# Edge places compared with the lanes on GpSimd, tile by tile behind the gathers, in a graph layer with a routed expert layer

## The chip, the cores and the metric

The kernel runs on one core of a Trainium2 chip. The metric is the device time of one execution in microseconds (us). The core has five engines that run side by side, each in its own program order: TensorE (PE in the profile), VectorE (DVE), ScalarE (ACT), GpSimd (POOL) and SyncE (SP, which here only issues DMAs).

## The reference

Inputs are 6,250 nodes `x` of 256 features, 100,000 edges (`src`, `dst`, sorted by `dst`, and two weights per edge), the weights of one graph layer and of eight experts, all float32. What the part around the change computes:

```python
h_fwd = h @ W_forward.T                 # h = layernorm(x); 64 features
h_rev = h @ W_reverse.T
messages = h_fwd[src] * direction[:, 0:1] + h_rev[src] * direction[:, 1:2]
scores = leaky_relu(einsum('ef,hf->eh', messages, attn))        # 4 heads
exp_scores = exp(scores - scores.max(axis=0))
sum_exp = segment_sum(exp_scores, dst)
norm = exp_scores / (sum_exp[dst] + 1e-10)
outs = [segment_sum(messages * norm[:, hd:hd + 1], dst) for hd in range(H)]
x = x + concatenation of outs           # 4 x 64 = 256 features
```

After it every node is normalized again, sent to one of eight experts by the largest of eight gate logits (with a limit on the nodes per expert), goes through a layer of 1,024 hidden units with ReLU, is weighted by its gate probability, and is added to `x`.

## The kernel before

**First stage (about 0 to 75 us).** The kernel normalizes the nodes, multiplies them by both weight matrices and stores a table of 6,250 rows of 136 floats in HBM (`node_tab`: for each direction 64 features and 4 head scores). It also transposes the edge data so that each column holds a tile of 128 edges, one per partition. `srci` holds the sources as integers; `local` holds, for each edge, the row of its destination within a window of up to 128 consecutive nodes (lines 813 and 814, through `less`). `lane` is a 128x128 tile with 0 to 127 along each row, and `lane_p` is a copy of it in PSUM, in the tile `fixed`.

**The edge stage (about 75 to 1170 us).** There are 782 edge tiles. They are taken in `NB` = 66 bursts of up to `GB` = 12 tiles, in the order of the list `order`. For each burst b:

- `gathers(b)` (line 985): one indirect DMA on GpSimd per tile (line 989) fetches 128 rows of `node_tab` into `gt`, which has three buffers. Between the gathers of a burst's second half it also issues scatters of routed rows (`put`, line 1198), if some are waiting in `pool_work`.
- `messages(b)` (line 995): VectorE multiplies both directions by their edge weights (lines 1004 and 1009), adds them (1011) and makes the scores; ScalarE takes the exponential (1024).
- `places(b)` (line 1027): VectorE compares `local` with the lanes, for all tiles of a burst in one instruction (line 1032). The result `hot` has a 1 where an edge's destination is that lane. It has two buffers.
- `products(b)` (line 1036): VectorE multiplies messages and exponentials for the four heads (line 1041).
- `windows(b, half)` (line 1052): PE multiplies `hot` with the products (line 1073), six tiles in each half, and accumulates in PSUM the sums for a window of nodes. ScalarE copies a finished window out (line 1077) and SyncE stores it into `sums`.

**The order of the work** is written out by hand: the loop at line 1461 builds every engine's program in the order of its calls. In iteration b it calls `messages(b)`, `windows(b-1, 0)`, a share of expert work, `places(b)`, `products(b)`, `windows(b-1, 1)`, another share of expert work, and at the end `gathers(b+3)`. In between, `step_routing` advances the routing of chunks of nodes whose sums are complete: it loads the sums again (line 1105), divides, adds, normalizes (1114 to 1128), finds the expert and the slot, and leaves scatters to GpSimd. `step_experts` calls the expert matmuls (lines 1351 and 1369) by a fixed share of estimated costs, so that how much expert work stands in an iteration is settled when the program is built.

**The tail (to the end)**: the remaining expert matmuls, and the gathers and stores of the outputs.

Operands of VectorE's large instructions lie in PSUM on one side (`fixed`, `rv`), so most of them have a single input in SBUF.

Of the kernel before, what the change touches and what calls it, by code (L numbers as in the profile page):

```python
# [8 lines left out]
F32 = mybir.dt.float32  # L9
I32 = mybir.dt.int32  # L10
AF = mybir.ActivationFunctionType
OP = mybir.AluOpType
AX = mybir.AxisListType

P = 128
# [504 lines left out]
def kernel(  # L520
# [27 lines left out]
    nc = tc.nc  # L548
# [14 lines left out]
    ROW = 2 * MS  # L563
# [6 lines left out]
    GB = 12  # L570
# [10 lines left out]
    GT = GB // 2  # L581
# [24 lines left out]
    node_tab = dram.tile([N, ROW], F32, name="node_tab")  # L606
# [38 lines left out]
    lane = const.tile([P, P], F32, name="lane")  # L645
# [55 lines left out]
    srci = ep.tile([P, EW], I32, name="srci")  # L701
    ea = ep.tile([P, 2, EW], F32, name="ea")
    local = ep.tile([P, ET], F32, name="local")
# [153 lines left out]
    def clear(r):  # L857

        nc.sync.dma_start(buf[r:r + 512, 0:D].rearrange("(p n) d -> p n d", n=4),
                          zeros.rearrange("p (n d) -> p n d", n=4))  # L860

    def clear_last(e):

        r0, r1 = e * TOT + OFF[NP - 2], (e + 1) * TOT
        J = (r1 - r0) // P
        nc.sync.dma_start(ybuf[r0:r1, :].rearrange("(p n) d -> p (n d)", n=J), zeros[:, 0:J * D])
        r0 = e * TOT + OFF[NP - 1]
        J = (r1 - r0) // P
        nc.sync.dma_start(buf[r0:r1, D:BW].rearrange("(p n) k -> p n k", n=J),
                          zeros[:, 0:J * (D + 2)].rearrange("p (n k) -> p n k", k=D + 2))  # L870
# [7 lines left out]
    order = [(i, min(i + GB, TOP)) for i in range(HEAD, TOP, GB)]  # L878
# [3 lines left out]
    NB = len(order)  # L882
# [59 lines left out]
    with tc.tile_pool(name="p4", bufs=1) as p4, tc.tile_pool(name="p5", bufs=2) as p5, \  # L942
# [3 lines left out]
        p2 = edge_pools.enter_context(tc.tile_pool(name="p2", bufs=2))  # L946
# [4 lines left out]
        lane_p, shift_p = fixed[:, 0:P], fixed[:, P:P + H]  # L951

        def turn(b, k0, k1):
            o = P + H + b % 2 * (2 + H) * GB
            return fixed[:, o + k0 * GB:o + k1 * GB]
# [23 lines left out]
            got.append(over)  # L979


        gts, vs = {}, {}
        pool_work = []

        def gathers(b):
            i0, i1 = order[b]
            gts[b] = p2.tile([P, GB, ROW], F32, name="gt", bufs=3)
            for i in range(i0, i1):
                nc.gpsimd.indirect_dma_start(  # L989
                    out=gts[b][:, i - i0, :], out_offset=None, in_=node_tab,  # L990
                    in_offset=bass.IndirectOffsetOnAxis(ap=srci[:, i:i + 1], axis=0))
                if i - i0 >= GT and pool_work:
                    pool_work.pop(0)()

        def messages(b):

            i0, i1 = order[b]
            n = i1 - i0
            gt = gts.pop(b)
            m = p2.tile([P, GB, MS], F32, name="m")  # L1000
            fac = turn(b, 0, 2).rearrange("p (k j) -> p k j", k=2)
            nc.vector.tensor_copy(fac[:, :, :n], ea[:, :, i0:i1])
            fw = gt[:, :n, 0:MS]
            nc.vector.tensor_mul(fw, fw, fac[:, 0, :n].unsqueeze(2).to_broadcast([P, n, MS]))  # L1004
            for a0 in range(0, n, GT):
                a1 = min(a0 + GT, n)
                k = a1 - a0
                rv = ps2.tile([P, GT, MS], F32, name="rv")
                nc.vector.tensor_mul(rv[:, :k, :], gt[:, a0:a1, MS:ROW],  # L1009
                                     fac[:, 1, a0:a1].unsqueeze(2).to_broadcast([P, k, MS]))  # L1010
                nc.vector.tensor_add(m[:, a0:a1, :], fw[:, a0:a1, :], rv[:, :k, :])  # L1011
            sc = p2.tile([P, GB, H], F32, name="sc")
            s = sc[:, :n, :]
            nc.vector.scalar_tensor_tensor(s, m[:, :n, O:MS], 0.2, m[:, :n, O:MS],
                                           op0=OP.mult, op1=OP.max)
            if i1 == ET:
                nc.vector.tensor_scalar(sc[:, n - 1, :], sc[:, n - 1, :], no_edge, None, op0=OP.add)
            nc.vector.tensor_reduce(gmax[:, b, :], s.rearrange("p j h -> p h j"), AX.X, OP.max)
            if b == 0:
                nc.vector.tensor_reduce(shift, spread(gmax[:, 0, :]), AX.X, OP.max)  # L1020
                nc.vector.tensor_copy(shift_p, shift)
            nc.vector.tensor_sub(s, s, shift_p.unsqueeze(1).to_broadcast([P, n, H]))  # L1022
            v = p2.tile([P, GB, ACC], F32, name="v")
            nc.scalar.activation(v[:, :n, H * O:ACC], s, AF.Exp)  # L1024
            vs[b] = m, v

        def places(b):

            i0, i1 = order[b]
            n = i1 - i0  # L1030
            hot = p2.tile([P, GB, P], F32, name="hot")
            nc.vector.tensor_tensor(hot[:, :n, :], lane_p.unsqueeze(1).to_broadcast([P, n, P]),  # L1032
                                    local[:, i0:i1].unsqueeze(2).to_broadcast([P, n, P]), OP.is_equal)
            vs[b] += (hot,)

        def products(b):
            n = order[b][1] - order[b][0]
            m, v, hot = vs[b]
            w = turn(b, 2, 2 + H).rearrange("p (j h) -> p j h", h=H)
            nc.vector.tensor_copy(w[:, :n, :], v[:, :n, H * O:ACC])  # L1040
            nc.vector.tensor_mul(  # L1041
                v[:, :n, 0:H * O].rearrange("p n (h o) -> p n h o", h=H),
                m[:, :n, 0:O].unsqueeze(2).to_broadcast([P, n, H, O]),
                w[:, :n, :].unsqueeze(3).to_broadcast([P, n, H, O]))

            vl = p2.tile([P, ACC], F32, name="vl")
            nc.scalar.copy(vl, v[:, n - 1, :])  # L1047
            vs[b] = v, hot, vl

        taken = {"released": 0, "passes": 0, "before": None, "pv": None, "rows": 0, "jobs": 0, "fetched": 0}  # L1050

# [376 lines left out]
        def routes_of(c):  # L1428
            nonlocal next_p
            for cost in route(c, next_p):  # L1430
                yield cost
            if chunks[c][-1] == LASTS[next_p]:
                end_pass(next_p)
                wait_pass.append(next_p)
                next_p += 1
                if next_p < NP:
                    begin_pass(next_p)
                yield 0.0

        def step_routing():  # L1440
            nonlocal credit
            while routing:
                cost = next(routing[0], None)
                if cost is None:
                    routing.pop(0)
                    continue
                credit -= cost
                break

        def step_experts(share):  # L1450
            nonlocal credit
            credit = min(credit + share, share)
            while credit > 0 and b > 12:
                cost = step_ffn()
                if cost is None:
                    break
                credit -= cost

        for b in range(3):
            gathers(b)  # L1460
        for b in range(NB + 1):
            if 4 <= b < 4 + E:
                clear(1024 * (b - 4))
                clear(1024 * (b - 4) + 512)
                clear_last(b - 4)
            if b < NB:
                messages(b)
            step_routing()
            if b:
                windows(b - 1, 0)  # L1470
            step_experts(SHARE / 2)
            step_routing()
            if b < NB:
                places(b)
            step_routing()
            if b < NB:
                products(b)
            step_routing()
            if b:
                windows(b - 1, 1)  # L1480
            taken["released"] = taken["rows"]
            step_experts(SHARE / 2)
            while next_c < len(chunks) and done_at[next_c] < b:
                routing.append(routes_of(next_c))
                next_c += 1
            step_routing()
            pool_work.extend(todo)
            del todo[:]
            if b + 3 < NB:
                gathers(b + 3)  # L1490
            if wait_pass and not pool_work:
                taken["rows"] = wait_pass.pop() + 1
                i = (taken["rows"] - 1) * E
                if taken["jobs"] >= i - 1:
                    fetch_rows(i)
                    fetch_rows(i + 1)
# [115 lines left out]
```

## Time and profile before

| what | value |
| --- | --- |
| median of 9 runs | 1452.01 us (1445.87 to 1457.55) |
| the profiled execution | 1448.44 us |
| its span in the profile | 1446.6 us |
| PE busy | 1085.1 us (75%) |
| VectorE busy | 971.6 us (67%) |
| GpSimd busy | 863.2 us (60%) |
| ScalarE busy | 306.5 us (21%) |
| granted TensorE clock, mean | 0.85 of full speed |

How to read what follows. A group of instructions stands in one line: source line, engine, operation, what it writes and reads, the count behind an x, then its busy time in us and the mean of one in ns, then how long its engine was idle just before such instructions and what ended most of that idle time. "issue" means that the profile shows nothing that the engine waited for. In a timeline each line has the start, the duration, the engine and instruction, and in brackets the idle time before it. A row of the waits has who waited for whom, the sum in us, how often, and the longest. In the row of 40 slices each digit is the busy share of one slice of about 36 us, in tenths.

### The profile page before, as it was taken

The page shows a single profiled execution, that of the slowest core. Times are in us where ns is not written, and L with a number is a line of the kernel's source. Part 1 is how long each engine was busy: PE and PEld are TensorE (multiplying, and loading weights), DVE is VectorE, ACT ScalarE, POOL GpSimd, SP SyncE. Part 2 cuts the span into 40 slices and gives each one's busy share as a digit, 9 for nine tenths or more (in the row PEclk, how much of TensorE's full clock was granted, in tenths as well). Part 3 has the DMA queues.
Part 4 walks back from the last instruction along what each step waited for, and adds up shares of the span by engine and source line. Part 5 has one row for each costly group of instructions (what it writes and reads, how often), then busy time and mean ns, then how long its engine had stood idle before and what let it go on. Part 6 is the DMA issues. An engine that isn't in the chain of part 4 may idle for free.

```text
span 1446.6 us, 15046 instructions
## 1 busy us (share of the span) xinstructions
PE 1085.1 (75%) x4658; PEld 867.8 (60%) x4658; DVE 971.6 (67%) x2062; ACT 306.5 (21%) x771; POOL 863.2 (60%) x912
## 2 busy tenths in 40 slices
PE   6815554647447561979897998797889998999885
PEld 5614443435325341767676776675768887888774
DVE  6836557587578584576969878779789744215772
ACT  3500000010011010222222222222222233224441
POOL 0067777777777777767777777775777502004414
PEclk9957677767767666989898898898879999999998
DMA  7422666563333343448466675765675456767992
GB/s 226 130 51 63 176 187 187 152 188 76 75 104 71 80 110 97 130 134 217 131 189 174 185 193 157 172 195 150 169 187 157 141 171 197 259 200 253 298 290 73
DMA packets 160583, 231.22 MB, mean 160 GB/s; under 512 B 19760, under 2 KB 130542, under 8 KB 160366
## 3 DMA queue, kind: packets, MB, share of 16 engines
q1 hardware_dynamic: 125354, 152.34, 33.4%
q0 software_dynamic: 32064, 75.13, 21.7%
q10 hardware_dynamic: 3076, 2.69, 0.6%
q8 instruction: 39, 0.64, 0.2%
q14 instruction: 50, 0.41, 0.1%
HBM read 167.19 MB, written 63.70 MB: 160 GB/s over the span
## 4 chain that ended last, share of the span: by engine, by line
PE 31%; POOL 21%; DVE 19%; DMA 16%; issue 11%; ACT 2%; SPq 0%; DVEq 0%; POOLq 0%; ACTq 0%
POOL gt L989 19%; PE ph L1351 8%; PE pv L1073 8%; PE py L1369 8%; DVE v L1041 4%; DMA part<-sums 4%; DMA sums<-r 3%; DMA gt<-node_tab,srci 2%; PE pn L783 2%; PE pl L1142 2%; DMA out_dram<-o 1%; DVE hot L1032 1%; DMA yg<-ybuf,to_get 1%; DVE ln_st L673 1%; DVE hx L1122 1%
## 5 line engine op out<-in xcount | busy, mean ns | idle before, releaser
L989 POOL DMA_INDIRECT gt<-node_tab,srci x782 | 747.6, 956 | 257.4 <-issue 234.4
L1073 PE MATMUL pv<-v,hot 128*128 128x260 f32 x1564 | 459.7, 447 | 132.8 <-DVE v L1041 126.2
L1073 PEld LDWEIGHTS pv<-v,hot 128*128 128x128 f32 x1564 | 337.4, 224 | 237.5 <-issue 179.5
L1351 PE MATMUL ph<-xT,w1t 128*128 128x256 f32 x1024 | 237.8, 385 | 6.8 <-DVE y L1277 6.2
L1369 PE MATMUL py<-w2t,hf 128*128 128x256 f32 x1024 | 228.6, 380 | 4.2 <-ACT hf L1354 4.2
L1041 DVE TENSOR_TENSOR v<-m,fixed 128x3072 f32<-128x3072 f32 (+1 forms) x66 | 218.7, 3313 | 2.3
L1351 PEld LDWEIGHTS ph<-xT,w1t 128*128 128x128 f32 x1024 | 197.7, 194 | 36.4 <-DVE y L1277 7.4
L1369 PEld LDWEIGHTS py<-w2t,hf 128*128 128x128 f32 x1024 | 192.2, 190 | 30.9 <-ACT hf L1354 5.9
L1004 DVE TENSOR_TENSOR gt<-gt,fixed 128x816 f32<-128x816 f32 (+1 forms) x66 | 65.6, 993 | 151.7 <-DMA gt<-node_tab,srci 144.4
L1354 ACT ACTIVATE hf<-ph,b1t 128x256 f32<-128x256 f32 x256 | 105.9, 470 | 187.3 <-PE ph L1351 187.1
L1401 POOL DMA_INDIRECT yg<-ybuf,to_get x49 | 48.6, 992 | 151.3 <-DMA xr<-x_d 80.1
L1032 DVE TENSOR_TENSOR hot<-fixed,local 128x1536 f32<-128x1536 f32 (+1 forms) x66 | 114.2, 1730 | 0.0
L1134 PE MATMUL pt<-ident,hx 128*128 128x128 f32 x98 | 23.5, 413 | 90.2 <-DVE hx L683 90.2
L1198 POOL DMA_INDIRECT buf<-hx,to_put x49 | 48.5, 990 | 68.6 <-DVE kept L1219 44.4
L1277 DVE TENSOR_TENSOR y<-py,b2b 128x512 f32<-128x512 f32 x32 | 22.0, 686 | 94.2 <-PE py L1369 94.2
L1024 ACT ACTIVATE v<-sc 128x48 f32<-128x48 f32 (+1 forms) x66 | 16.0, 242 | 313.4 <-DVE sc L1022 313.3
L1011 DVE TENSOR_TENSOR m<-gt,rv 128x408 f32<-128x408 f32 x131 | 75.5, 576 | 4.5
L1009 DVE TENSOR_TENSOR rv<-gt,fixed 128x408 f32<-128x408 f32 x131 | 76.1, 581 | 2.2
L1047 ACT COPY vl<-v 128x260 f32<-128x260 f32 x66 | 26.9, 407 | 235.6 <-DVE v L1041 175.6
L1134 PEld LDWEIGHTS pt<-ident,hx 128*128 128x128 f32 x98 | 17.9, 210 | 95.8 <-DVE hx L683 57.2
L1077 ACT COPY r<-pv 128x260 f32<-128x260 f32 x87 | 32.2, 370 | 115.6 <-PE pv L1073 115.6
L1142 PEld LDWEIGHTS pl<-gw,ht 128*128 128x128 f32 x196 | 42.5, 328 | 2.8 <-ACT ht L1136 2.7
(221 smaller groups left out, 894.3 us busy)
## 6 DMA issues: line engine op xcount, KB each, us to landing
w1t<-in_L_ffn_w_dram SPq DMA_DIRECT2D x32, 1024.0 KB
w2t<-in_L_ffn_w_dram SPq DMA_DIRECT2D x32, 1024.0 KB
gt<-node_tab,srci POOLq DMA_INDIRECT x782, 2.9
sums<-r SPq DMA_DIRECT2D x85, 125.9 KB
buf<-zeros SPq DMA_DIRECT2D x16, 512.0 KB
xe<-buf SPq DMA_DIRECT2D x32, 256.0 KB
part<-sums SPq DMA_DIRECT2D x12, 520.0 KB
x_d<-hx SPq DMA_DIRECT2D x12, 512.0 KB
```

Of the source, the lines that this page charges most:

```text
L989: nc.gpsimd.indirect_dma_start(out=gts[b][:, i - i0, :], out_offset=None, in_=node_tab, in_offset=bass.IndirectOffsetOnAxis(ap=srci[:, i:i ...
L1004: nc.vector.tensor_mul(fw, fw, fac[:, 0, :n].unsqueeze(2).to_broadcast([P, n, MS]))
L1009: nc.vector.tensor_mul(rv[:, :k, :], gt[:, a0:a1, MS:ROW], fac[:, 1, a0:a1].unsqueeze(2).to_broadcast([P, k, MS]))
L1011: nc.vector.tensor_add(m[:, a0:a1, :], fw[:, a0:a1, :], rv[:, :k, :])
L1032: nc.vector.tensor_tensor(hot[:, :n, :], lane_p.unsqueeze(1).to_broadcast([P, n, P]), local[:, i0:i1].unsqueeze(2).to_broadcast([P, n, P]) ...
L1041: nc.vector.tensor_mul(v[:, :n, 0:H * O].rearrange("p n (h o) -> p n h o", h=H), m[:, :n, 0:O].unsqueeze(2).to_broadcast([P, n, H, O]), w[ ...
L1073: nc.tensor.matmul(pv, hot[:, i - i0, :], v[:, i - i0, :], start=(i == g0), stop=(i == g1 - 1))
L1142: nc.tensor.matmul(pl[:, n, :], hts[n // 2][:, n % 2, d, :], gw[:, d, :], start=(d == 0), stop=(d == DC - 1))
L1351: nc.tensor.matmul(ph[:, f - f0, :], w1t[:, d, f * P:(f + 1) * P], xT[:, d, :S], start=(d == 0), stop=(d == DC - 1))
L1354: nc.scalar.activation(hf[:, f, :S], ph[:, f - f0, :], AF.Relu, bias=b1t[:, e * FC + f:e * FC + f + 1])
L1369: nc.tensor.matmul(py[:, j - j0, :], hf[:, f, j * P:(j + 1) * P], w2t[:, f, :], start=(f == 0), stop=(f == FC - 1))
L1401: nc.gpsimd.indirect_dma_start(out=yg[:, n, :], out_offset=None, in_=ybuf, in_offset=bass.IndirectOffsetOnAxis(ap=to_get[:, n0 + n:n0 + n ...
```

## The change

The comparison moves from VectorE to GpSimd. It is split into one instruction per tile, which reads `lane` from SBUF and one column of `local` as a scalar per partition. The comparisons of burst b-1 stand in `gathers(b)`, one behind each gather, so the places of a burst are made while the next burst is gathered. The tile `hot` gets four buffers in place of two. `gathers` is called one more time, with b = `NB`, for the places of the last burst alone. The call of `places` in the main loop goes, and `products` takes the places from a dictionary of their own.

```diff
         def gathers(b):
-            i0, i1 = order[b]
-            gts[b] = p2.tile([P, GB, ROW], F32, name="gt", bufs=3)
-            for i in range(i0, i1):
-                nc.gpsimd.indirect_dma_start(
-                    out=gts[b][:, i - i0, :], out_offset=None, in_=node_tab,
-                    in_offset=bass.IndirectOffsetOnAxis(ap=srci[:, i:i + 1], axis=0))
-                if i - i0 >= GT and pool_work:
-                    pool_work.pop(0)()
+            i0, i1 = order[b] if b < NB else (0, 0)
+            if b < NB:
+                gts[b] = p2.tile([P, GB, ROW], F32, name="gt", bufs=3)
+            for i in range(GB):
+                if i < i1 - i0:
+                    nc.gpsimd.indirect_dma_start(
+                        out=gts[b][:, i, :], out_offset=None, in_=node_tab,
+                        in_offset=bass.IndirectOffsetOnAxis(ap=srci[:, i0 + i:i0 + i + 1], axis=0))
+                    if i >= GT and pool_work:
+                        pool_work.pop(0)()
+                if b:
+                    places(b - 1, i)
...
-        def places(b):
+        def places(b, i):
             i0, i1 = order[b]
-            n = i1 - i0
-            hot = p2.tile([P, GB, P], F32, name="hot")
-            nc.vector.tensor_tensor(hot[:, :n, :], lane_p.unsqueeze(1).to_broadcast([P, n, P]),
-                                    local[:, i0:i1].unsqueeze(2).to_broadcast([P, n, P]), OP.is_equal)
-            vs[b] += (hot,)
+            if not i:
+                places_of[b] = p2.tile([P, GB, P], F32, name="hot", bufs=4)
+            if i < i1 - i0:
+                nc.gpsimd.tensor_scalar(places_of[b][:, i, :], lane, local[:, i0 + i:i0 + i + 1], None, op0=OP.is_equal)
...
-            vs[b] = v, hot, vl
+            vs[b] = v, places_of.pop(b), vl
...
-            if b < NB:
-                places(b)
...
-            if b + 3 < NB:
+            if b + 3 <= NB:
                 gathers(b + 3)
```

More of the change, by code (lines that the diff above doesn't have):

```diff
@@ L979, in term @@
             got.append(over)
-        gts, vs = {}, {}
+        gts, vs, places_of = {}, {}, {}
         pool_work = []
         def gathers(b):
-            i0, i1 = order[b]
-            gts[b] = p2.tile([P, GB, ROW], F32, name="gt", bufs=3)
-            for i in range(i0, i1):
-                nc.gpsimd.indirect_dma_start(
-                    out=gts[b][:, i - i0, :], out_offset=None, in_=node_tab,
-                    in_offset=bass.IndirectOffsetOnAxis(ap=srci[:, i:i + 1], axis=0))
-                if i - i0 >= GT and pool_work:
-                    pool_work.pop(0)()
+            i0, i1 = order[b] if b < NB else (0, 0)
[10 more added lines that the diff above has]
+                    places(b - 1, i)
         def messages(b):
@@ L1025, in messages @@
             vs[b] = m, v
-        def places(b):
+        def places(b, i):
             i0, i1 = order[b]
-            n = i1 - i0
-            hot = p2.tile([P, GB, P], F32, name="hot")
-            nc.vector.tensor_tensor(hot[:, :n, :], lane_p.unsqueeze(1).to_broadcast([P, n, P]),
-                                    local[:, i0:i1].unsqueeze(2).to_broadcast([P, n, P]), OP.is_equal)
-            vs[b] += (hot,)
+            if not i:
+                places_of[b] = p2.tile([P, GB, P], F32, name="hot", bufs=4)
+            if i < i1 - i0:
+                nc.gpsimd.tensor_scalar(places_of[b][:, i, :], lane, local[:, i0 + i:i0 + i + 1], None, op0=OP.is_equal)
         def products(b):
             n = order[b][1] - order[b][0]
-            m, v, hot = vs[b]
+            m, v = vs[b]
             w = turn(b, 2, 2 + H).rearrange("p (j h) -> p j h", h=H)
```

## The prediction

> **What bounds the kernel now.** I read the busy row of GpSimd over the 40 slices first, then the costliest groups, then GpSimd's own timeline, and last the waits, because the change puts 782 new instructions on one engine and the question is whether that engine has room.
>
> From the page: the slices, and the two groups that the change touches.
> ```profile
> POOL 0067777777777777767777777775777502004414
> ...
> L989 POOL DMA_INDIRECT gt<-node_tab,srci x782 | 747.6, 956 | 257.4 <-issue 234.4
> ...
> L1032 DVE TENSOR_TENSOR hot<-fixed,local 128x1536 f32<-128x1536 f32 (+1 forms) x66 | 114.2, 1730 | 0.0
> ```
> GpSimd is only about 75% busy from slice 3 to slice 29, which looks like room. The gather row says what the other quarter is: of 257.4 us idle ahead of the gathers, 234.4 are "issue", time in which the engine waited for nothing that the profile shows. The timeline of GpSimd alone shows its form (start, duration, idle before):
> ```profile
> 77.36 0.95 POOL L989 DMA_INDIRECT gt<-node_tab,srci  x1 [0.30 <-issue]
> 78.62 0.94 POOL L989 DMA_INDIRECT gt<-node_tab,srci  x1 [0.30 <-issue]
> 79.86 0.94 POOL L989 DMA_INDIRECT gt<-node_tab,srci  x1 [0.30 <-issue]
> ```
> A gather starts every 1.25 us, 0.94 busy and 0.30 between, and the same 0.30 stands ahead of nearly every later gather. It belongs to the gather; it is not slack. The first gather starts at 75.90 and the last (1144.13 + 0.95) ends at 1145.08: a stage of 1069.2 us. In it lie 782 gathers (747.6 us) and 48 scatters of routed rows (47.5 us), and between those 830 instructions 829 gaps of 0.30 (about 250 us). That leaves 1069.2 - 795.1 - 250 = 24 us in which GpSimd waited for anyone. The engine is full for the whole stage.
>
> Who waits for it: VectorE, whose first instruction of a burst (L1004) waits on gathered rows, in this row of the waits:
> ```profile
> DVE gt L1004 <- DMA gt<-node_tab,srci: 144.4, 25, 20.6
> ```
> The stretches 600 to 850 and 850 to 1150 us of the table by windows show that the other engines come close without being the limit:
> ```profile
> 600.00:850.00 250.00, 223.86 (x971) 173.92 (x970) 197.99 (x423) 59.35 (x142) 183.61 (x191) 0.90 0.61 166
> 850.00:1150.00 300.00, 267.34 (x1171) 217.06 (x1170) 250.81 (x534) 69.73 (x165) 214.53 (x223) 0.90 0.63 174
> ```
> (columns: length; PE, PE's weight loads, DVE, ACT, POOL; clock; DMA). PE is at 89 to 90%, DVE at 79 to 84%. The page's chain of work that ended last gives only "POOL gt L989 19%", but a chain follows the last releaser of each step; the rate of the stage is set by the engine that never pauses. After 1145 us the tail, 1446.6 - 1145.1 = 301.5 us, is PE working off an order fixed when the program was built.
>
> **What the change removes.** 66 VectorE comparisons, 114.2 us by the row of L1032. VectorE waits 144.4 us for gathered rows as it is, so this makes its idle time longer and shortens nothing as long as gathers come at GpSimd's pace. I book zero. If that cover were gone, that is if VectorE set the pace, it would be worth up to 1.73 us a burst.
>
> **What it adds.** 782 comparisons on GpSimd, one behind each gather, 128x128 f32, each with a per-partition scalar operand. The trace has none on GpSimd. Nearest rows of the GpSimd groups:
> ```profile
> masks.py:199 POOL TENSOR_SCALAR_AFFINE_SELECT ident<-ident 128x128 f32<-128x128 f32 x1 | 0.3, 283 | 0.0
> ...
> L624 POOL MEMSET upto<- 128x128 f32 x1 | 0.2, 202 | 0.0
> L641 POOL TENSOR_SCALAR_AFFINE_SELECT no_edge<-no_edge 128x1 f32<-128x1 f32 x1 | 0.2, 176 | 0.0
> ...
> L640 POOL MEMSET no_edge<- 128x1 f32 x1 | 0.1, 88 | 0.0
> ```
> The affine select reads a 128x128 tile, compares and writes it, so it is the nearest. Its duration is 0.28; the two that run back to back start at 1.21 and 1.45 us, so one occupies the engine for 0.24. I take 0.26, between the two. The scalar operand is one more thing to read: at 128x1, where the length costs nothing, the form that reads takes 176 - 88 = 0.09 us more than the one that only writes, and I add 0.075, rounded down because part of that difference is the comparing. So one comparison is 0.335 us, and 782 of them are 262 us.
>
> Bounds of that cost. From below: the comparison runs in the 0.30 us ahead of the next gather, which leaves 0.03, or nothing. From above: the comparison needs a gap of 0.30 of its own, 0.335 + 0.30 = 0.635, times 782 = 497 us. I stay at 0.335, because the small GpSimd instructions at the start follow one another with an idle time of 0.0; the gap shows only with indirect DMAs, and their number is unchanged.
>
> **What moves.** The places of burst b are now made during the gathers of b+1 instead of on VectorE right after its messages. So the first half of PE's matmuls of burst b (L1073) comes when GpSimd is halfway through the next burst, and the second half at its end. Queued behind these matmuls on PE are the expert matmuls of that iteration and the routing's transposes, and the sums that routing loads. With 12 x (1.25 + 0.335) = 19 us a burst against 15, PE (13.5 us of 15) has 5 us to spare each time, and nothing piles up. GpSimd's new wait is for a free buffer of places, last read by matmuls four bursts back; behind it would stand all later gathers, but PE has finished those bursts before, so zero; one missed wait would cost a part of a 15 us burst. The wait on the local places costs nothing: the last of them is written at 62 us (L807), before any gather. The scatters stand where they stood, between gathers of the second half of a burst, each now with a comparison behind it. At the end, an extra pass makes the last 10 places with no gather: 10 x 0.335 = 3.4 us, already in the 782, and beside the last messages, which take from 1147 to 1155 us now. The PE tail of 301.5 us has the same order and stays.
>
> The 24 us of GpSimd's waits become partly free, since everyone else gets more time per burst: I take half, -12.
>
> **Contention, a rule that speaks against the change.** In the trace a gather takes 944 ns in the median and 956 on average, so 782 x 12 ns = 9 us is all that disturbs GpSimd now; I book nothing more.
>
> The Trainium skill ("SBUF — State Buffer", section "Who interferes with whom") says that a VectorE instruction with two inputs in SBUF shuts out a GpSimd instruction that reads SBUF until it is done, and that is the kind that is added. Nothing in this trace tests it. By that rule the two-input instructions of the stage (L1121, L1122, L1281, L1014: 14.7 + 14.7 + 9.9 + 13.6 = 53 us, 5% of the stage) would stop some 40 of the 782 comparisons for half a microsecond each, an estimate of 20 us more.
>
> **The sum.** 262 - 12 = +250 us. The profiled execution took 1448.4 us (span 1446.6 and 1.8 around it), which gives 1698; against the median of the nine runs, 1452.0, it is 1702. I give the latter.
>
> **Rivals.**
> 1. Each comparison brings a gap of its own (0.635 us a tile). For it: the 0.30 stands ahead of every indirect DMA, whatever came before, and no row shows what stands behind one when another kind of instruction follows. Against: the idle time of 0.0 between plain instructions. Time: 1452 + 497 - 24 = 1925. A chance of 0.24.
> 2. Not slower: the comparison runs inside the 0.30. Place: the gap ahead of the next gather. Price: 0 to 0.03 us a tile. It decides from the point at which a comparison of 0.335 or less starts as soon as the gather's busy time ends and the next gather's preparation goes on beside it, so that the 1.25 us pitch remains. Then GpSimd's stage keeps its 1069 us less at most the 24 us of waits, VectorE's 114 us only add slack, and the time is 1428 to 1452. For it: nothing shows who spends the 0.30. Against: if that preparation could go on beside another instruction, it should already go on beside the gather before it. A chance of 0.08.
> 3. Changing between two kinds of instruction is dear. The very first gather, after three iotas, started 1.2 us after its semaphore event (74.7 to 75.90) and took 1.15 instead of 0.94. If each alternation cost that, 0.9 + 0.2 + 0.335 = 1.4 us a tile, 1100 us in all, about 2550. Against: it is one instance, and it was also the first gather of all. A chance of 0.04.
>
> That the change does not move the comparison at all is ruled out, since the diff names the engine.
>
> **How the numbers follow.** My forecast (0.335 us a tile, from 0.18 to 0.45 with its unknowns: 1590 to 1800) has 0.64, the rivals 0.24, 0.08 and 0.04. The range must reach the first rival, and leaves out the second and third and the edges: 1590 to 1930. Within 0.3% is what a measurement of this kernel can tell from no change. Faster by more: 0.05 (most of rival 2); within: 0.03; slower by more: 0.92.
>
> **What would show it.** GpSimd's timeline in the stage should show gather and comparison in turn, the pitch 1.25 + 0.335, idle time ahead of a comparison near 0 and ahead of a gather still 0.30. A pitch of 1.9 is rival 1, of 1.25 rival 2. The last gather should end near 1395 us and the tail after it stay near 300. VectorE's row for L1032 is gone and its wait for gathered rows (144.4) grows by some hundreds of us. I am wrong if the stage grows but the tail shrinks (then PE had work to bring forward), or if GpSimd waits for the buffers of places or for PE.

## The result, and the profile after

The changed kernel takes 1899.25 us (median of 10 runs, 1897.39 to 1905.83), against 1450.64 us of the kernel before (31 runs). The ratio is 1.3093, 95% interval 1.307 to 1.3115. The profiled execution took 1908.35 us, with a span of 1906.5, longer than any of the ten. The loss is 449 us by the medians (460 between the two profiled executions), where 250 were forecast: the time lies inside the range of 1590 to 1930, but not near its middle, and nearer to the first rival's 1925 than to 1702.

From the page of the changed kernel: GpSimd's slices, and the costliest groups of the two engines concerned.
```profile
POOL 0388888888888888888888888888888888110333
...
L992 POOL DMA_INDIRECT gt<-node_tab,srci x782 | 812.8, 1039 | 144.8 <-issue 142.9
...
L1038 POOL TENSOR_SCALAR hot<-lane,local 128x128 f32<-128x128 f32 x782 | 502.6, 643 | 26.4
L1009 DVE TENSOR_TENSOR gt<-gt,fixed 128x816 f32<-128x816 f32 (+1 forms) x66 | 65.5, 993 | 669.1 <-DMA gt<-node_tab,srci 576.6
```
The block of sevens on GpSimd has become a longer block of eights. One comparison takes 643 ns, and little idle time stands ahead of it (26.4 us in all). VectorE's wait for gathered rows ahead of L1009, the old L1004, has grown from 144.4 to 576.6 us: VectorE was given time off and spends it waiting for gathers.

GpSimd's timeline in the middle of the stage, with start, duration and idle time before:
```profile
480.19 0.63 POOL L1038 TENSOR_SCALAR hot<-lane,local 128x128 f32<-128x128 f32 x1
480.99 1.03 POOL L992 DMA_INDIRECT gt<-node_tab,srci  x1 [0.17 <-issue]
482.06 0.63 POOL L1038 TENSOR_SCALAR hot<-lane,local 128x128 f32<-128x128 f32 x1
482.85 1.03 POOL L992 DMA_INDIRECT gt<-node_tab,srci  x1 [0.17 <-issue]
```
The pitch, from the start of one gather to the start of the next, is 1.87 us. The gather with all that belongs to it is about as long as before: 0.04 idle ahead of the comparison, 0.17 ahead of the next gather, and the gather's own 1.03 make 1.24, against 0.30 + 0.94. The other 0.63 is the comparison itself.

The same timeline at the end of the stage:
```profile
1609.12 1.03 POOL L992 DMA_INDIRECT gt<-node_tab,srci  x1 [0.17 <-issue]
1610.19 7.58 POOL L1038 TENSOR_SCALAR hot<-lane,local 128x128 f32<-128x128 f32 x13
```
The first gather starts at 75.72 and the last ends at 1610.15: a stage of 1534.4 us, 465.2 more than before. The tail after it is 1906.5 - 1610.15 = 296.4 us, 5 less. So the whole loss of the profiled execution lies in the gather stage. The last line also gives a price with no gather between: 13 comparisons in a row take 7.58 us, 0.583 each.

The waits of the changed kernel have a new row that could tell another story:
```profile
PE pv L1077 <- POOL hot L1038: 219.5, 122, 8.2
PE pt L1138 <- DVE hx L683: 169.9, 12, 42.0
```
PE now waits 219.5 us for the places, and its wait for the rows that routing normalizes (second row) has grown from 90.2 us. Either that is only PE standing idle because GpSimd has become slower, or the places, made one burst late, hold PE up and are a cause of their own.

### The profile page after: what moved, and what is told of

The parts are those of the page before. It is cut to its first block, busy times and chain, and to the rows that moved or that the text cites. A ratio compares the mean times of both kernels' runs of the same rounds, so it can differ in the third digit from the quotient of the medians.

```text
span 1906.5 us, 15788 instructions
## 1 busy us (share of the span) xinstructions
PE 1204.6 (63%) x4658; PEld 895.9 (47%) x4658; DVE 880.0 (46%) x1996; ACT 304.2 (16%) x771; POOL 1432.1 (75%) x1694
## 4 chain that ended last, share of the span: by engine, by line
POOL 63%; PE 12%; issue 10%; DMA 8%; DVE 6%; ACT 1%; SPq 0%; POOLq 0%; DVEq 0%; ACTq 0%
POOL gt L992 37%; POOL hot L1038 23%; PE ph L1355 4%; PE py L1373 3%; POOL buf L1202 2%; DMA out_dram<-o 2%; PE pn L783 1%; PE pv L1077 1%; DMA gt<-node_tab,srci 1%; DMA sums<-r 1%; DMA yg<-ybuf,to_get 1%; DMA buf<-hx,to_put 1%; DVE v L1045 1%; DVE o L1319 1%; DMA part<-sums 1%
## 5 line engine op out<-in xcount | busy, mean ns | idle before, releaser
L992 POOL DMA_INDIRECT gt<-node_tab,srci x782 | 812.8, 1039 | 144.8 <-issue 142.9
L1077 PE MATMUL pv<-v,hot 128*128 128x260 f32 x1564 | 551.5, 499 | 294.8 <-POOL hot L1038 219.5
L1077 PEld LDWEIGHTS pv<-v,hot 128*128 128x128 f32 x1564 | 358.5, 245 | 470.9 <-POOL hot L1038 308.7
L1038 POOL TENSOR_SCALAR hot<-lane,local 128x128 f32<-128x128 f32 x782 | 502.6, 643 | 26.4
L1009 DVE TENSOR_TENSOR gt<-gt,fixed 128x816 f32<-128x816 f32 (+1 forms) x66 | 65.5, 993 | 669.1 <-DMA gt<-node_tab,srci 576.6
L1355 PE MATMUL ph<-xT,w1t 128*128 128x256 f32 x1024 | 245.3, 394 | 10.8 <-DVE y L1281 7.8
L1355 PEld LDWEIGHTS ph<-xT,w1t 128*128 128x128 f32 x1024 | 202.5, 199 | 43.2 <-DVE y L1281 9.4
L1014 DVE TENSOR_TENSOR rv<-gt,fixed 128x408 f32<-128x408 f32 x131 | 76.1, 581 | 2.3
L1269 PE MATMUL px<-ident,xe 128*128 128x128 f32 x128 | 21.1, 292 | 64.3 <-DMA xe<-buf 63.5
L1269 PEld LDWEIGHTS px<-ident,xe 128*128 128x128 f32 x128 | 17.1, 153 | 70.0 <-DMA xe<-buf 52.0
```

What stands on the lines that cost most here:

```text
L992: nc.gpsimd.indirect_dma_start(out=gts[b][:, i, :], out_offset=None, in_=node_tab, in_offset=bass.IndirectOffsetOnAxis(ap=srci[:, i0 + i:i ...
L1014: nc.vector.tensor_mul(rv[:, :k, :], gt[:, a0:a1, MS:ROW], fac[:, 1, a0:a1].unsqueeze(2).to_broadcast([P, k, MS]))
L1038: nc.gpsimd.tensor_scalar(places_of[b][:, i, :], lane, local[:, i0 + i:i0 + i + 1], None, op0=OP.is_equal)
L1077: nc.tensor.matmul(pv, hot[:, i - i0, :], v[:, i - i0, :], start=(i == g0), stop=(i == g1 - 1))
L1355: nc.tensor.matmul(ph[:, f - f0, :], w1t[:, d, f * P:(f + 1) * P], xT[:, d, :S], start=(d == 0), stop=(d == DC - 1))
```

## The theories

**A.** A comparison occupies GpSimd for its own time, GpSimd sets the pace of the stage, and nothing else matters. Then the forecast's mechanism stands, and only the size of one comparison was wrong.

**B.** A part of the loss comes from the placement: the places are ready later, PE waits for them, and what is queued behind on PE and VectorE comes later.

**C.** Alternating is what is dear: any instruction between two indirect DMAs costs about 0.6 us (the first rival's gap, or the third's change of instruction).

A further question is which part of the comparison is dear: the operand per partition, the comparing, or the elements.

## Experiments: the comparison by itself

Six kernels keep the kernel before as it is, with VectorE's places, and put one more GpSimd instruction behind each gather, which writes a spare tile that nobody reads. No place is later and no engine waits for them.

```diff
                 if i - i0 >= GT and pool_work:
                     pool_work.pop(0)()
+                nc.gpsimd.tensor_scalar(spare, lane, local[:, i:i + 1], None, op0=OP.is_equal)   # d_ts128
+                nc.gpsimd.tensor_scalar(spare[:, 0:16], lane[:, 0:16], ..., op0=OP.is_equal)     # d_ts16
+                nc.gpsimd.tensor_scalar(spare[:, 0:64], lane[:, 0:64], ..., op0=OP.is_equal)     # d_ts64
+                nc.gpsimd.tensor_scalar(spare, lane, 5.0, None, op0=OP.is_equal)                 # d_imm128
+                nc.gpsimd.tensor_scalar(spare, lane, local[:, i:i + 1], None, op0=OP.mult)       # d_mul128
+                nc.gpsimd.affine_select(out=spare, in_=lane, compare_op=OP.is_ge, ...)           # d_aff128
```
(one of the lines in each kernel)

**d_ts128, the same comparison, unused.** 

> The kernel before, with VectorE still making the places, and behind each gather the same GpSimd comparison (lane against one column of local) into a spare tile that nobody reads. Theory A (the comparison's own busy time is added to GpSimd's pitch, and that is all): pitch 1.87 us, time within 1% of the changed kernel, 1885 to 1915 us. Theory B (a part of the loss comes from PE waiting for places that are made later): PE has nothing new to wait for here, so the time stays clearly below, 1700 to 1850 us.

Measured: 1909.94 us, ratio 1.3126 (1.3102 to 1.3151), against 1.3093 (1.307 to 1.3115) for the change. Its groups on GpSimd:
```profile
L991 POOL DMA_INDIRECT gt<-node_tab,srci x782 | 813.8, 1041 | 135.0 <-issue 133.8 <-DVE least L1120 0.2 <-DVE carry L1176 0.2
L996 POOL TENSOR_SCALAR spare<-lane,local 128x128 f32<-128x128 f32 x782 | 498.2, 637 | 27.1
```
The same gathers, the same comparisons and, by the ratio, the same time, though PE waits for none of these comparisons. What PE waits for in their place, against 126.2 us for the same products before:
```profile
PE pv L1076 <- DVE v L1044: 307.6, 28, 19.9
```
Theory B falls: PE idles as much without late places (219.5 + 74.4 us for places and products in the changed kernel), now behind VectorE's products, which wait for gathered rows. Its wait for the rows of the routing is 188.5 us here, so that doesn't need late places either. The 219.5 us of PE's new wait are PE idling at GpSimd's pace. VectorE's 114 us of comparisons are still there in this kernel and cost next to nothing, which is the other side of the forecast's zero.

**d_ts16, 16 lanes.** 

> As d_ts128, but the comparison covers 16 of the 128 lanes. If the price is by the element, the comparison costs some 0.15 us and the time is near 1560 us; if it is a fixed price of issuing another kind of instruction between two indirect DMAs (theory C), it stays above 0.5 us a tile, 1830 us or more.

Measured: 1696.58 us, ratio 1.1661 (1.164 to 1.1682). Its timeline:
```profile
299.28 1.03 POOL L991 DMA_INDIRECT gt<-node_tab,srci  x1 [0.17 <-issue]
300.35 0.34 POOL L996 TENSOR_SCALAR spare<-lane,local 128x16 f32<-128x16 f32 x1
300.86 1.03 POOL L991 DMA_INDIRECT gt<-node_tab,srci  x1 [0.17 <-issue]
```
A pitch of 1.58: 0.33 more than a gather alone. Neither of the two expectations holds; it is half and half. There is a fixed part and a part by the element.

**d_ts64, 64 lanes.** 

> As d_ts128, but 64 of the 128 lanes. The pitches of 16 and 128 lanes, 1.58 and 1.87 us, give 0.29 us fixed and 2.6 ns an element over the 1.25 of a gather. If that is a straight line, 64 lanes have a pitch of 1.70 and the time is 1790 us, plus or minus 20. If only the overlap with the gap makes the small one cheap, the pitch is 1.75 or more, 1825 us or more.

Measured: 1792.35 us, ratio 1.2335 (1.2298 to 1.2372). Its timeline:
```profile
300.93 1.03 POOL L991 DMA_INDIRECT gt<-node_tab,srci  x1 [0.17 <-issue]
302.00 0.47 POOL L996 TENSOR_SCALAR spare<-lane,local 128x64 f32<-128x64 f32 x1
302.63 1.03 POOL L991 DMA_INDIRECT gt<-node_tab,srci  x1 [0.17 <-issue]
```
The pitch is 1.70, on the straight line. One comparison costs 0.29 us and 2.6 ns an element on top of a gather: 0.29 + 128 x 0.0026 = 0.62.

**d_imm128, a constant in place of the operand per partition.** 

> As d_ts128, but lane is compared with the constant 5.0, with no per-partition operand. The prediction gave that operand 0.075 us. If the operand is the dear part, the comparison falls to about 0.3 us and the time to about 1680 us; if it is cheap, as the prediction had it, about 0.55 us a tile stay and the time is 1840 us or more.

Measured: 1936.14 us, ratio 1.3308 (1.3283 to 1.3332), slower than with the operand. Its timeline:
```profile
300.35 1.03 POOL L991 DMA_INDIRECT gt<-node_tab,srci  x1 [0.27 <-issue]
301.45 0.54 POOL L996 TENSOR_SCALAR spare<-lane 128x128 f32<-128x128 f32 x1
302.25 1.03 POOL L991 DMA_INDIRECT gt<-node_tab,srci  x1 [0.27 <-issue]
```
The instruction reads 0.54 in place of 0.63, as the forecast's 0.075 for the operand would have it. But the gap ahead of the next gather is 0.27 in place of 0.17, and the pitch is 1.90. A duration in GpSimd's rows is not the price; the pitch is. The operand is not the dear part.

**d_mul128, a product in place of the comparison.** 

> As d_ts128, but lane is multiplied with the column of local in place of compared. If the comparing itself is the dear part of the instruction, the pitch falls to that of an affine select, 1.42 us, near 1580 us. If the form (two operands per element through GpSimd's tensor-with-scalar code) is what costs, nothing changes: 1890 to 1925 us.

Measured: 1891.02 us, ratio 1.3016 (1.2977 to 1.3054). Its timeline:
```profile
301.00 1.01 POOL L991 DMA_INDIRECT gt<-node_tab,srci  x1 [0.17 <-issue]
302.05 0.62 POOL L996 TENSOR_SCALAR spare<-lane,local 128x128 f32<-128x128 f32 x1
```
A pitch of 1.84. The comparing is not the dear part either: another operation in the same form of instruction (a tile and a scalar, TENSOR_SCALAR in the trace) costs nearly the same.

**d_aff128, the row that the forecast took as nearest.** 

> As d_ts128, but behind each gather stands the instruction that the prediction took as its nearest row, an affine select over 128x128 that reads lane and writes the spare tile. Theory A: it costs what it costs at the start of the kernel, 0.24 to 0.28 us, with the gather's gap unchanged: 1640 to 1670 us. Theory C (alternating with gathers is dear for any instruction): 0.6 us a tile, about 1900 us.

Measured: 1576.55 us, ratio 1.0837 (1.0817 to 1.0857), less than either theory gave. Its timeline:
```profile
300.71 0.30 POOL L996 TENSOR_SCALAR_AFFINE_SELECT spare<-lane 128x128 f32<-128x128 f32 x1
301.17 0.95 POOL L991 DMA_INDIRECT gt<-node_tab,srci  x1 [0.16 <-issue]
302.13 0.30 POOL L996 TENSOR_SCALAR_AFFINE_SELECT spare<-lane 128x128 f32<-128x128 f32 x1
302.59 0.94 POOL L991 DMA_INDIRECT gt<-node_tab,srci  x1 [0.16 <-issue]
```
The pitch is 1.42: an instruction of 0.30 us adds 0.17, because the gap ahead of the gather shrinks from 0.30 to 0.16. Theory C falls: alternating is not dear, here it even hides 0.13 us. The affine select over the same 128x128 numbers adds 0.17 where the comparison adds 0.62. What inside the TENSOR_SCALAR form makes it dearer, these runs do not show.

| kernel | pitch by its trace, us | over 1.25 | times 782, us | measured growth of the time, us |
| --- | --- | --- | --- | --- |
| d_aff128 | 1.42 | 0.17 | 133 | 122 |
| d_ts16 | 1.58 | 0.33 | 258 | 242 |
| d_ts64 | 1.70 | 0.45 | 352 | 341 |
| d_mul128 | 1.84 | 0.59 | 461 | 439 |
| d_ts128 | 1.87 | 0.62 | 485 | 455 |
| d_imm128 | 1.90 | 0.65 | 508 | 481 |

(the last column: its median less that of the kernel before in the same session.) In each, the time grows by the added pitch times the number of gathers, less 11 to 30 us. GpSimd's waits, 24 us before, can be most of that difference; the pitches are read to 0.01 us, which is 8 us in this column. GpSimd's pitch sets the time of the stage.

## Experiments: the change in parts

**a_dve, the change with its comparisons on VectorE.**
```diff
-                nc.gpsimd.tensor_scalar(places_of[b][:, i, :], lane, ...
+                nc.vector.tensor_scalar(places_of[b][:, i, :], lane, ...
```


> The changed kernel with its placement, its split into one comparison per tile and its four buffers, but with the 782 comparisons on VectorE in place of GpSimd. If GpSimd's occupancy is the whole loss, GpSimd is back at 1.25 us a gather and the time is within 1% of the kernel before, 1440 to 1465 us. If the late placement or the split costs something by itself, it stays above 1480 us.

Measured: 1457.62 us, ratio 1.0051 (1.0037 to 1.0064). Its comparisons, one per tile:
```profile
L1038 DVE TENSOR_SCALAR hot<-lane,local 128x128 f32<-128x128 f32 x782 | 161.7, 296 | 2.7 <-DMA node_tab<-nt 2.7
```
They take 161.7 us of VectorE against 114.2 in one instruction per burst. GpSimd waits a little more for others, the last gather ends at 1155.1 instead of 1145.1, and that is about the half per cent. Split, placement and buffers together are small; the engine is the loss.

**a_half, every second comparison on VectorE.**
```diff
-                nc.gpsimd.tensor_scalar(places_of[b][:, i, :], lane, ...
+                (nc.vector if i % 2 else nc.gpsimd).tensor_scalar(places_of[b][:, i, :], lane, ...
```


> The changed kernel with every second comparison of a burst on VectorE. GpSimd then has 391 comparisons at 0.62 us: if the loss is linear in their number, 1450 + 391 x 0.62 - 12 = 1680 us, plus or minus 20. If alternating is what costs, or if waits of PE make up part of it, it is not half: above 1750 or below 1600 us.

Measured: 1667.47 us, ratio 1.1493 (1.1472 to 1.1514). Its timeline shows both prices side by side:
```profile
302.06 1.03 POOL L992 DMA_INDIRECT gt<-node_tab,srci  x1 [0.17 <-issue]
303.39 0.95 POOL L992 DMA_INDIRECT gt<-node_tab,srci  x1 [0.30 <-issue]
304.38 0.62 POOL L1038 TENSOR_SCALAR hot<-lane,local 128x128 f32<-128x128 f32 x1
305.18 1.03 POOL L992 DMA_INDIRECT gt<-node_tab,srci  x1 [0.17 <-issue]
```
A gather behind a gather starts 1.33 us after it, one behind a comparison 1.79; the two together take 3.12 us, which is 1.25 + 1.87. Half the comparisons give 217 of 449 us. The loss is linear in their number.

**a_late, the comparisons of a burst behind its last gather.**
```diff
-                if b:
-                    places(b - 1, i)
+            for i in range(GB if b else 0):
+                places(b - 1, i)
```


> The changed kernel with the comparisons of a burst in a row behind its last gather, in place of one behind each gather. The 13 comparisons that the changed kernel runs in a row at its end take 0.583 us each, and gathers in a row have a pitch of 1.25. Theory A: 1.83 us a tile in place of 1.87, 15 to 35 us less than the changed kernel, 1865 to 1885 us. Theory C (alternation is dear): 100 us less or more, 1800 us or below.

Measured: 1871.7 us, ratio 1.2905 (1.2882 to 1.2927), as theory A has it. Its timeline:
```profile
323.67 0.94 POOL L992 DMA_INDIRECT gt<-node_tab,srci  x1 [0.30 <-issue]
324.92 0.94 POOL L992 DMA_INDIRECT gt<-node_tab,srci  x1 [0.30 <-issue]
325.89 4.66 POOL L1038 TENSOR_SCALAR hot<-lane,local 128x128 f32<-128x128 f32 x8
```
The comparisons take 0.583 us each in a row, and the gathers are back at 1.25. Bundling saves 27 us of the loss, no more.

**b_deep, an attempt to go below the kernel before.** It keeps VectorE's comparisons and is meant to take away GpSimd's last waits.
```diff
-            gts[b] = p2.tile([P, GB, ROW], F32, name="gt", bufs=3)
+            gts[b] = p2.tile([P, GB, ROW], F32, name="gt", bufs=4)
...
-        for b in range(3):
+        for b in range(4):
             gathers(b)
...
-            if b + 3 < NB:
-                gathers(b + 3)
+            if b + 4 < NB:
+                gathers(b + 4)
```


> The kernel before with four buffers of gathered rows in place of three and the gathers called one burst earlier. It takes away GpSimd's remaining waits, 24 us in the gather stage by the trace of before, if those waits are for buffers or for late rows to scatter. Theory A (GpSimd sets the pace): 1430 to 1445 us. If PE or VectorE sets the pace of the second half, or if later scatters hold up the experts, no gain or a loss: 1448 us or more.

Measured: 1469.4 us, ratio 1.0123 (1.0104 to 1.0141): 1.2% slower. A fourth buffer did not take the waits away: GpSimd still waits for VectorE's L1014 (12.2 us, against 10.0), and the last gather ends at 1148.5 instead of 1145.1. So this run doesn't test what the stage would gain without those waits. Most of the loss comes behind the gathers, where the last scatter waits longer for VectorE:
```profile
POOL buf L1198 <- DVE kept L1219: 59.5, 1, 59.5
```
It was 44.4 us. The last scatter starts at 1207.97 instead of 1189.49 and the span is 20.8 us longer. That the late scatter holds up the experts fits these numbers, but was not tried by itself, and why it comes later is open. No kernel here beats the kernel before.

## Why the prediction was right and where it was wrong

- **GpSimd is full, and its 0.30 is not slack.** Right in the main, and all rests on it: the cost of every kind of instruction that was put on GpSimd came out in the time (table above). But 0.13 of the 0.30 can be used: d_aff128's instruction of 0.30 adds 0.17.
- **VectorE's 114.2 us are worth nothing.** Right: without them (the change) and with them (d_ts128) the ratio is 1.309 and 1.313.
- **One comparison costs 0.335 us.** Wrong, and this is the step that failed. It costs 0.62 between gathers and 0.583 in a row. The affine select was taken for it since it reads, compares and writes as many numbers; d_aff128 shows that the two are priced apart, 0.17 against 0.62 on the pitch. The step took the shape of the work as the price and left the instruction's own form out. In the stage 769 comparisons (13 come behind it) x 0.62 = 477 us stand where the forecast had 262. The forecast's own spread for this term ended at 0.45 us, or 1800 us, and the measured time is beyond it.
- **The gap.** The forecast left it unchanged; in truth the idle time ahead of a gather falls to 0.17, with 0.04 ahead of the comparison, but the gather itself reads 1.03, so the sum stays at 1.24.
- **The first rival** gave nearly the right time for a wrong reason. It wanted a second gap of 0.30 ahead of the comparison; there is 0.04. A pitch of 1.9 was to be its sign, and 1.87 came without that gap. The upper bound of the cost that it brought (0.635) is what made the range hold. That the time lies inside the range is luck: the bound stood for a gap that did not come.
- **The second rival**, hiding in the gap, does exist in part for an affine select, which hides 0.13 of its 0.30. A comparison of 0.63 adds 0.62.
- **The third rival**, a dear change of instruction, is out: an affine select between gathers adds 0.17 (d_aff128), and bundling the comparisons saves only 27 us (a_late).
- **What moves.** Right: GpSimd has no new wait of any size, PE follows, and the tail is 296.4 us against 301.5. The 0.5% of a_dve is what split, placement and buffers cost together, with VectorE making the places.
- **Waits given back: -12.** The balance fits: the stage grew by 465.2, against 477 for comparisons. But more than waits is in it. The idle time of GpSimd beyond the usual gap, added up over the stage, falls by 17 us (from 21.5 to 4.4), and comparisons that take longer than most cost some 10 us (last section).
- **Contention.** The forecast booked none, and gave 20 us as an estimate by the rule that it cites. Comparisons beside VectorE instructions with two inputs in SBUF took 8 us more in all. The forecast's word that nothing in the trace of the kernel before tests the rule is wrong where gathers are concerned; see the last section.

## What to carry to other kernels

Look at the pitch of an engine's instructions and not at its busy share: here an engine that read 75% busy, with a fixed gap ahead of each instruction, was full, and a comparison added there was paid in full (an affine select a little over half). Freeing an engine that waited anyway gained nothing. For an operation that the trace doesn't show, the price of an instruction of the same shape and another form can be far off (0.17 against 0.62 here): keep a wide upper bound in the range, and measure the operation unused beside the old kernel, as d_ts128 did in one run.

## What the runs showed of the hardware that was not expected

**GpSimd's tensor-with-scalar instruction** costs 0.29 us and 2.6 ns an element over a gather's pitch (16, 64 and 128 elements a partition). At 128 elements a product costs nearly the same as a comparison (0.59 and 0.62), and with a constant operand the pitch is even 0.03 longer. The affine select over 128 elements adds 0.17.

**Beside some of VectorE's instructions, comparisons and gathers take longer.** The Trainium skill ("SBUF — State Buffer", section "Who interferes with whom") has it that a VectorE instruction with two inputs in SBUF shuts out a GpSimd instruction that reads SBUF. The changed kernel's timeline, both engines, where VectorE runs such instructions (L1125 and L1126):
```profile
1043.29 1.71 POOL L1038 TENSOR_SCALAR hot<-lane,local 128x128 f32<-128x128 f32 x1
1043.31 1.23 DVE L1125 TENSOR_TENSOR part<-part,den 128x1024 f32<-128x1024 f32 x1
1044.57 1.26 DVE L1126 TENSOR_TENSOR hx<-hx,part 128x1024 f32<-128x1024 f32 x1
1045.17 1.57 POOL L992 DMA_INDIRECT gt<-node_tab,srci  x1 [0.17 <-issue]
```
The comparison takes 1.71 in place of 0.63 and ends 0.46 us after L1125 does, and the gather beside L1126 takes 1.57 in place of 1.03. In the stage 26 comparisons took over 0.70 us; together they are 10 us over 0.63 each. Of these, 19 lie beside instructions that read two tiles in SBUF (L1125, L1126, L1285), with 8 of the 10 us, against the forecast's estimate of 20. The other 7 lie beside L683, which reads one tile and two scalars per partition, so two inputs are not the whole of it.

The kernel before shows the same for gathers, beside the same two instructions (there L1121 and L1122):
```profile
422.50 1.22 DVE L1121 TENSOR_TENSOR part<-part,den 128x1024 f32<-128x1024 f32 x1
422.75 1.79 POOL L989 DMA_INDIRECT gt<-node_tab,srci  x1 [0.30 <-issue]
423.76 1.23 DVE L1122 TENSOR_TENSOR hx<-hx,part 128x1024 f32<-128x1024 f32 x1
```
Each of the 12 times that this pair runs in the stage, one gather takes 1.41 to 1.79 us in place of 0.94. The runs show the coincidence; no run took VectorE's instructions away.

**The granted TensorE clock** was lower in the changed kernel, where PE had less to do: 0.768 on average against 0.85, and the same 4658 matmuls were busy for 1204.6 us against 1085.1. The stretch from 600 to 850 us, for which the prediction shows 223.86 us of PE and a clock of 0.90, now reads:
```profile
600.00:850.00 250.00, 124.85 (x405) 81.39 (x404) 96.91 (x201) 22.13 (x58) 221.28 (x263) 0.67 0.28 73
```
What lowered the clock was not tried. It doesn't show in the time: the stage goes at GpSimd's pace, and the tail is no longer than before.
